# Letting the first gathers of a layer depend on 30 of 32 units' rows

## The chip, the cores and the metric

One core of a Trainium2 chip runs the whole program. TensorE (PE) multiplies matrices; its weight loads are listed apart as PEld. VectorE (DVE), ScalarE (ACT) and GpSimd (POOL) do the rest, and SyncE (SP) and POOL issue DMAs, which 16 DMA engines carry out. Each engine works through its own instruction list in the order in which the program was written. The metric is the time of one execution on the device, in microseconds (us).

## The reference

`x` holds 8 graphs' features for the same 2048 nodes, 128 numbers per node. `adj` says which nodes are neighbours; it is sparse: 34928 of the 2048 x 2048 entries are set, about 17 per node. Four layers follow each other: attention with 8 heads, graph attention, attention, graph attention.

```python
# attention layer, per node n over its neighbours m
scores = einsum('bnhd,bmhd->bhnm', Q, K) / sqrt(16);  scores = where(adj == 0, -inf, scores)
x = layer_norm(h + softmax(scores) @ V @ Wo + bo);  x = layer_norm(x + relu(x @ W1 + b1) @ W2 + b2)
# graph layer
h = x @ W;  e = leaky_relu((h @ a_src)[:, :, None] + (h @ a_dst)[:, None, :]);  e = where(adj == 0, -inf, e)
x = layer_norm(x + softmax(e) @ h)
```

A node's result in one layer needs the previous layer's result of all its neighbours.

## The kernel before, in words

**Units and slots.** The nodes are cut into 32 units of 64 nodes, each unit into two groups of 32. The edges of a group are written one per slot. A unit has nine tiles of 128 slots: four pairs of tiles (one tile of each pair per group, `t` = 0 to 3) and a shared ninth tile (`t` = 4), which takes what a group has beyond 512 edges, the first group from the front and the second from the back. `block_list` and `unit_list` (from L1027 and L1108) build these lists from `adj` on the chip: for each slot the index of the neighbour (`idx`), the node that owns it (`owner`) and a one-hot matrix (`hot`). An unused slot gets an index outside the table and is skipped. If a list overflows, the program runs a dense version (`failed`, `net`).

**Tables.** After a unit has finished a layer, `project` (L1390) makes its rows for the next layer: keys and values for attention, projected features for a graph layer. `store` (L1464) writes them to that layer's table in DRAM, a DMA that SP issues (L1470; L1467 for layer 0). `gather` (L1540) then fetches, by POOL's indirect DMAs (L1547), the rows of the slots of one unit's tile; a pair of tiles takes two such DMAs. Each gather reads the whole table, so the first gather of a layer waits for the stores of all 32 units.

**Attention layer** (`attention`, L1569), per unit and tile: PE spreads queries to slots (`qe`, L1620), DVE multiplies with the gathered keys (L1632) and sums (L1639), ACT takes the exponential (L1649), POOL or DVE multiplies the values with it (L1658), PE adds per node (L1690). `after_attention` is the rest of the layer: a chain of products, normalisations and transpositions. **Graph layer** (`graph`, L1790): PE spreads the nodes' scores to slots (`ps_te`, L1803), DVE adds the gathered ones (L1866, L1873), ACT takes the exponential (L1878), DVE makes weights (L1888), PE adds (L1904) into a bank `q` for even units and into `acc` and `sums` for odd ones. `after_graph` is the rest.

**Buffers.** `kv` (gathered rows) has 6 buffers, each of which holds one pair's gathers in an attention layer and four gathers in a graph layer; `hot` has 3, `te` 2, `x` 4. In PSUM there are one `q`, one `acc`, one `sums` and two `m`. The last unit of a layer is worked on in two halves (`in_halves`, L1701); `bank` (L1331) takes `m` for the first half and the `q` bank for the second.

**Order.** No engine's order is written out. Every step is an `op` with a cost per engine, a key and the cells that it reads and writes. `Plan.order` (L666) plays the program through with these costs and writes the instructions down in the order in which it started them; among steps that are ready on an engine the lowest key goes first. Layer n's keys begin at 1000 n, a unit adds 5, a tile 1; gathers are 6 or 12 lower than the tile that they serve. `kv`, `hot`, `x`, `q_sb` and `acc` are handed out strictly in order of keys (`BY_KEY`, L53): a later step can't take a buffer before an earlier one has.

Of the kernel before, what the change touches and what calls it, by code (L numbers as in the profile page):

```python
# [9 lines left out]
F32 = mybir.dt.float32  # L10
# [10 lines left out]
P = 128  # L21
H = 8
# [19 lines left out]
WIDE = DEG + 5  # L42
QB = 4
# [7 lines left out]
    "cand": 2, "aux": 3, "unit_aux": 2, "some": 2, "rank_e": 2, "pick": 1,  # L51
}
# [712 lines left out]
class Sparse:  # L765
# [15 lines left out]
    def __init__(self, ctx, tc, x, xt, xk, adj, w, out):  # L781
# [22 lines left out]
        self.late = False  # L804
# [13 lines left out]
        self.table = [Cell() for _ in LAYERS]  # L818

# [12 lines left out]
        self.ends = self.const.tile([P, self.NU, 2], F32, name="ends")  # L832

# [13 lines left out]
    def constants(self):  # L847
# [67 lines left out]
        for p in range(2):  # L915
            nc.gpsimd.memset(self.same_unit[p * UNIT : (p + 1) * UNIT, p * UNIT : (p + 1) * UNIT], 1.0)
        self.middle = const.tile([P, P], F32, name="middle")
# [109 lines left out]
    def block_list(self, adj, i):  # L1027
# [38 lines left out]
        aux = cell("aux", [P, WIDE])  # L1066
        some = cell("some", [P, DEG])

        def largest(e):
            c = cand.tile.rearrange("p q c -> p (q c)")  # L1070
            for r in range(DEG // 8):
                top = aux.tile[:, 8 * r : 8 * r + 8]
                e.max(out=top, in_=c)
                if r < DEG // 8 - 1:
                    e.match_replace(out=c, in_to_replace=top, in_values=c, imm_value=0.0)
            e.tensor_scalar(
                some.tile, aux.tile[:, 0:DEG], 0.0, 0.0, ALU.is_gt, ALU.add, accum_out=aux.tile[:, DEG + 4 : WIDE]
            )
            e.tensor_reduce(self.seen[:, 1, i : i + 1], aux.tile[:, 0:DEG], axis=mybir.AxisListType.X, op=ALU.add)

# [3 lines left out]
        def places(e):  # L1084
            deg = aux.tile[:, DEG + 4 : WIDE]
            for c, (w, x) in enumerate(
# [5 lines left out]
                    (self.upto, deg),  # L1092
                    (self.same_unit, deg),
# [6 lines left out]
        def ends(e):  # L1100
            e.copy(aux.tile[:, DEG : DEG + 4], ps.tile[:, 0:4])
            e.copy(self.seen[:, 2:4, i], ps.tile[:, 4:6])

        op({"ACT": 0.45}, ends, key + 0.3, reads=[ps], writes=[aux])
        for p in range(2):
            self.unit_list(2 * i + p, p, aux, key + 5 * p)

    def unit_list(self, u, p, block_aux, key):  # L1108
        op, cell = self.op, self.cell
        ps = cell("m", [P, CH], name="ps_aux")  # L1110
        aux = cell("unit_aux", [P, 2, DEG + 3])
        ends = Cell()
# [4 lines left out]
            lambda e: e.matmul(ps.tile[:, 0:WIDE], lhsT=self.to_unit[p], rhs=block_aux.tile, start=True, stop=True),  # L1117
# [7 lines left out]
        def split(e):  # L1125
# [3 lines left out]
            e.mul(ends.tile[:, 1:2], ps.tile[:, DEG + 4 : WIDE], 0.5)  # L1129

# [15 lines left out]

        ps_l = cell("m", [P, 2 * TG, DEG + 3], name="ps_l")

        def parts(e):
            for t in range(TG):  # L1150
# [6 lines left out]
                )  # L1157
            e.matmul(
# [7 lines left out]
        op({"PE": 1.0}, parts, key, reads=[hot, aux], writes=[ps_l])  # L1166
# [57 lines left out]
    def parts(self, u):  # L1224

        for hf in range(2):
            yield slice(hf * UNIT, (hf + 1) * UNIT), slice(u * UNIT, (u + 1) * UNIT), hf

# [29 lines left out]
    def fetch(self, n, u, key):  # L1258
# [39 lines left out]
        )  # L1298
        self.op(
# [13 lines left out]
    def in_half(self, v, made):  # L1313

        self.blocks, self.made, self.at, self.plan.share = range(2 * v, 2 * v + 2), made, 0, 0.55
# [5 lines left out]
    def rows(self, tag, shape, axis, unit, name=None):  # L1321
# [3 lines left out]
        if self.at == len(self.made):  # L1325
            self.made.append(self.cell(tag, shape, name=name))
        cut = (slice(None),) * axis + (slice(self.blocks.start * unit, self.blocks.stop * unit),)
        self.at += 1
        return Part(self.made[self.at - 1], lambda t: t[cut])

    def bank(self, name, shape=None):  # L1331

        shape = shape or [P, len(self.blocks) * P]
        if self.made is None or not self.blocks.start:
# [55 lines left out]
    def project(self, n, u, x, key, of=None, shares=()):  # L1390
# [73 lines left out]
        def store(e):  # L1464
# [8 lines left out]
            {"SP": 0.9 if n else 0.45}, store, key, reads=[rows], joins=[self.table[n]], dma=P * half * 4  # L1473
# [66 lines left out]
    def gather(self, n, u, t, width, key, kv, rows, writes, shares=()):  # L1540

        tiles = 1 if t == TG - 1 else 2

        def start(e):
            for j in range(tiles):
# [4 lines left out]
                    in_=self.tables[n],  # L1550
                    in_offset=bass.IndirectOffsetOnAxis(ap=self.idx[:, u, col : col + 1], axis=0),
                    bounds_check=self.N - 1,
# [7 lines left out]
            reads=[self.table[n], self.idx_at[u]],  # L1560
# [8 lines left out]
    def attention(self, n):  # L1569
# [3 lines left out]
        for u in range(self.NU):  # L1573
            base = n * STRIDE + u * TG
            x, hot = self.fetch(n, u, base - 12)
            ps = cell("m", [P, CH], name="ps_q")

            def queries(e, ps=ps, x=x):
                for b in range(hb):
                    cols = slice(b * P, (b + 1) * P)  # L1580
                    e.matmul(ps.tile[:, cols], lhsT=x.tile[:, cols], rhs=L["Wq"], start=True, stop=True)

            q = cell("q_sb", [P, CH])
            op({"PE": 1.1}, queries, base - 4, reads=[x, self.weights_at[n]], writes=[ps], holds=[q])
            op({"ACT": 0.6}, lambda e, q=q, ps=ps: e.copy(q.tile, ps.tile), base - 4, reads=[ps], writes=[q])
            acc = cell("acc", [P, CH])
            sums = cell("sums", [P, hb * H])
            for t in range(TG):
                key = base + t
                kv = cell("kv", [P, KV])  # L1590
                self.gather(
                    n,
                    u,
                    t,
                    2 * width,
                    key - 6,
                    kv,
                    lambda kv, j: kv[:, j * 2 * width : (j + 1) * 2 * width],
                    writes=[kv],
                )  # L1600

                tiles = 1 if t == TG - 1 else 2


                def part(kv, k, tiles=tiles):
                    rows = kv.tile[:, 0 : tiles * 2 * width].rearrange("p (q k c) -> p q k c", k=2, c=CH)
                    return rows[:, :, k, :]

                def exps(kv, tiles=tiles):
                    return kv.tile[:, 4 * width : 4 * width + tiles * heads]  # L1610

                qe = cell("q", [P, 2, 2, CH], name="qe")

                def spread(e, t=t, qe=qe, q=q, hot=hot, tiles=tiles):
                    for j in range(tiles):
                        for hf in range(2):
                            at = (2 * hf + j) * GROUP

                            rows = slice(at, at + GROUP * (3 - tiles))
                            e.matmul(  # L1620
                                qe.tile[:, j, hf, :],
                                lhsT=hot.tile[rows, t * P : (t + 1) * P],
                                rhs=q.tile[rows, :],
                                start=True,
                                stop=True,
                            )

                op({"PE": 1.2}, spread, key - 6, reads=[q, hot, self.table[n]], writes=[qe])

                def multiply(e, kv=kv, qe=qe, part=part, tiles=tiles):  # L1630
                    k = part(kv, 0)
                    e.tensor_tensor(k, qe.tile[:, 0:tiles].rearrange("p j h c -> p (j h) c"), k, ALU.mult)  # L1632

                op({"DVE": 1.12 * tiles}, multiply, key, reads=[qe], writes=[kv])
                s = cell("s", [P, 2 * heads])

                def reduce(e, kv=kv, s=s, part=part, tiles=tiles):
                    k = part(kv, 0).rearrange("p q (c d) -> p q c d", d=HD)
                    e.tensor_reduce(  # L1639
                        s.tile[:, 0 : tiles * heads].rearrange("p (q c) -> p q c", q=2 * tiles),  # L1640
                        k,
                        axis=mybir.AxisListType.X,
                        op=ALU.add,
                    )

                op({"DVE": 1.12 * tiles}, reduce, key, reads=[kv], writes=[s])

                def exp(e, out, s=s, tiles=tiles):
                    e.activation(out, s.tile[:, 0 : tiles * heads], AF.Exp, scale=HD**-0.5)  # L1649

                op({"ACT": 0.32}, lambda e, kv=kv, exp=exp, exps=exps: exp(e, exps(kv)), key - 4, reads=[s], writes=[kv])

                by_vector = t == TG - 1 and (n or u % 2) or n and u % 4 == 0 and t == 2

                def weigh(e, kv=kv, w=None, part=part, exps=exps, tiles=tiles):
                    v = part(kv, 1).rearrange("p q (c d) -> p q c d", d=HD)
                    w = (exps(kv) if w is None else w[:, 0 : tiles * heads]).rearrange("p (q c) -> p q c", q=2 * tiles)
                    e.tensor_tensor(v, v, w.unsqueeze(3).to_broadcast([P, 2 * tiles, heads // 2, HD]), ALU.mult)  # L1658

                if by_vector:  # L1660
                    ps = cell("m", [P, CH], name="ps_e")
                    op(
                        {"ACT": 0.32},
                        lambda e, ps=ps, exp=exp, tiles=tiles: exp(e, ps.tile[:, 0 : tiles * heads]),
                        key - 4,
                        reads=[s],
                        writes=[ps],
                    )
                    op(
                        {"DVE": 1.14 * tiles},  # L1670
                        lambda e, kv=kv, ps=ps, weigh=weigh: weigh(e, kv, ps.tile),
# [406 lines left out]
```

## Time and profile before

| what | value |
|---|---|
| median of 3 runs | 3018.71 us (3015.15 to 3028.6) |
| the profiled execution | 3037.61 us, span 3035.9 us, mean granted PE clock 0.882 |
| busy share of the span | PE 78%, DVE 76%, POOL 70%, PE weight loads 47%, ACT 46% |
| moved by DMA | 1022.92 MB, mean 337 GB/s |
| POOL's indirect gathers | 1152, of 1037 ns mean on POOL |
| first gather of layers 0, 1, 2, 3 | at 130.84, 1188.73, 1661.90, 2598.85 us |
| table stores of L1470, L1467 | 192 DMAs (two per unit), 32 DMAs |

Busy time is from one profiled execution; a share over the whole span averages over layers with different limits. A number in square brackets after an instruction in the timeline is the time for which its engine stood still before it, with what ended that.

### The profile page before, as it was taken

The numbers are of one execution on the slowest core, as the hardware profiler recorded it, in microseconds if no ns is written. First come the engines' busy times: TensorE is split into PE (matmuls) and PEld (weight loads), VectorE is DVE, ScalarE is ACT, GpSimd is POOL, SyncE is SP. The second block draws the span as 40 slices with busy tenths as digits, with TensorE's granted clock in tenths as the row PEclk, the third lists the DMA queues.
The fourth block names the chain that finished last, engine by engine and source line by source line (L and its number), as shares of the span: only waits on it lengthen the run. The fifth ranks groups of instructions, "written<-read, shape, count | busy, mean of one in ns | idle before, by whom it ended". The sixth has DMA issues, their size and how long they took to land. (4 is left out here: it accounts for less than half of the span.)

```text
span 3035.9 us, 60069 instructions
## 1 busy us (share of the span) xinstructions
PE 2383.0 (78%) x22044; PEld 1429.6 (47%) x22044; DVE 2306.6 (76%) x3744; ACT 1409.6 (46%) x4789; POOL 2139.0 (70%) x1455
## 2 busy tenths in 40 slices
PE   7877888788888786888886778878888878677775
PEld 6633444444433334666664233334334334566664
DVE  6788999987897785555553988888988988566665
ACT  4635554445544442555553234444445434344453
POOL 1277887687888773766663878878887885577774
PEclk8779998899998887899889799999999999777787
DMA  7778889798898884999997988988989885799996
GB/s 286 290 281 334 345 320 344 301 344 303 329 339 337 306 309 142 406 409 404 394 408 279 372 322 352 382 348 349 369 353 364 339 347 222 285 402 407 399 399 256
DMA packets 248494, 1022.92 MB, mean 337 GB/s; under 512 B 39232, under 2 KB 53312, under 8 KB 176288
## 3 DMA queue, kind: packets, MB, share of 16 engines
q0 software_dynamic: 166464, 864.44, 73.5%
q1 hardware_dynamic: 81728, 154.55, 14.0%
q8 instruction: 177, 2.90, 0.4%
q14 instruction: 125, 1.02, 0.1%
HBM read 978.59 MB, written 88.08 MB: 351 GB/s over the span
## 5 line engine op out<-in xcount | busy, mean ns | idle before, releaser
L1547 POOL DMA_INDIRECT kv<-table,idx x1152 | 1194.6, 1037 | 700.9 <-issue 314.3
L1658 POOL TENSOR_TENSOR kv<-kv 128x2048 f32<-128x2048 f32 (+1 forms) x260 | 931.2, 3595 | 55.2 <-ACT kv L1649 51.2
L1632 DVE TENSOR_TENSOR kv<-qe,kv 128x2048 f32<-128x2048 f32 (+1 forms) x320 | 662.3, 2070 | 169.1 <-DMA kv<-table,idx 110.8
L1639 DVE TENSOR_REDUCE s<-kv 128x128 f32<-128x2048 f32 (+1 forms) x320 | 660.0, 2062 | 7.6 <-DVE kv L1632 0.5
L1620 PE MATMUL qe<-q_sb,hot 32*128 32x512 f32 (+1 forms) x2304 | 399.3, 694 | 204.3 <-DVE kv L1632 202.0
L1690 PE MATMUL acc<-kv,hot 128*32 128x512 f32 (+1 forms) x2304 | 372.6, 660 | 60.0 <-POOL kv L1658 43.9
L1904 PE MATMUL acc_q<-kv,w 128*32 128x129 f32 (+1 forms) x4608 | 219.8, 328 | 134.7 <-DVE w L1888 104.9
L1888 DVE TENSOR_TENSOR w<-hot,e 128x512 f32<-128x512 f32 (+1 forms) x384 | 221.3, 598 | 52.8 <-ACT e L1878 52.0
L1620 PEld LDWEIGHTS qe<-q_sb,hot 32*128 32x128 f32 (+1 forms) x2304 | 106.9, 196 | 327.1 <-DVE kv L1632 269.1
L1904 PEld LDWEIGHTS acc_q<-kv,w 128*32 128x32 f32 (+1 forms) x4608 | 171.5, 135 | 172.3 <-DVE w L1888 100.1
L1649 ACT ACTIVATE kv<-s 128x128 f32<-128x128 f32 (+1 forms) x320 | 95.1, 298 | 336.7 <-DVE s L1639 225.9
L1866 DVE TENSOR_TENSOR e<-te,kv 128x16 f32<-128x16 f32 (+1 forms) x320 | 58.9, 184 | 227.5 <-DMA kv<-table,idx 225.1
L1484 ACT ACTIVATE junk<-ps_c 128x128 f32<-128x128 f32 x492 | 136.1, 277 | 162.8 <-PE ps_c L1372 137.0
L1348 ACT COPY trows<-ps_p 128x512 f32<-128x512 f32 (+1 forms) x238 | 113.3, 478 | 190.1 <-PE ps_p L1412 102.0
L1690 PEld LDWEIGHTS sums<-kv,hot 128*32 128x32 f32 (+1 forms) x2304 | 90.3, 121 | 215.3 <-issue 212.8
L1878 ACT ACTIVATE e<-e 128x16 f32<-128x16 f32 (+1 forms) x320 | 66.7, 212 | 248.2 <-DVE e L1873 246.1
L1904 PE MATMUL acc<-kv,w 128*32 128x129 f32 (+1 forms) x2304 | 119.9, 309 | 76.7 <-DVE w L1888 70.1
L1372 PE MATMUL ps_c<-centre,r 128*128 128x128 f32 x1008 | 150.8, 295 | 28.8 <-DVE r L1740 18.4
L1372 PEld LDWEIGHTS ps_c<-centre,r 128*128 128x128 f32 x1008 | 130.1, 201 | 73.2 <-DVE r L1740 36.7
L1382 PE MATMUL ps_f<-x,W 128*128 128x512 f32 (+1 forms) x256 | 149.2, 667 | 13.0 <-ACT x L1527 9.1
L1690 PEld LDWEIGHTS acc<-kv,hot 128*32 128x32 f32 (+1 forms) x2304 | 55.4, 115 | 203.6 <-issue 106.2
L1770 PE MATMUL ps_y<-hidden,W 128*128 128x512 f32 (+1 forms) x256 | 144.8, 652 | 5.9 <-ACT hidden L1760 3.0
(205 smaller groups left out, 4038.4 us busy)
## 6 DMA issues: line engine op xcount, KB each, us to landing
x<-xd SPq DMA_DIRECT2D x96, 256.0 KB
xd<-xnew SPq DMA_DIRECT2D x93, 256.0 KB
kv<-table,idx POOLq DMA_INDIRECT x1152
table<-trows SPq DMA_DIRECT2D x128, 130.0 KB
kv<-adj_dram SPq DMA_DIRECT2D x16, 1024.0 KB
table<-trows SPq DMA_DIRECT2D x32, 512.0 KB
table<-trows SPq DMA_DIRECT2D x64, 256.0 KB
kv<-xk_dram SPq DMA_DIRECT2D x8, 1024.0 KB
```

What stands on the lines that cost most here:

```text
L1372: e.matmul(ps.tile[:, cols], lhsT=flat(x.tile)[:, cols], rhs=self.centre, start=True, stop=True)
L1382: lambda e: e.matmul(ps.tile, lhsT=w, rhs=x.tile, start=True, stop=True),
L1484: e.activation(self.junk, x, AF.Square, scale=P**-0.5, accum_out=var.tile[:, b, 1:2])
L1547: e.indirect_dma_start(out=rows(kv.tile, j), out_offset=None, in_=self.tables[n], in_offset=bass.IndirectOffsetOnAxis(ap=self.idx[:, u, co ...
L1620: e.matmul(qe.tile[:, j, hf, :], lhsT=hot.tile[rows, t * P : (t + 1) * P], rhs=q.tile[rows, :], start=True, stop=True,)
L1632: e.tensor_tensor(k, qe.tile[:, 0:tiles].rearrange("p j h c -> p (j h) c"), k, ALU.mult)
L1639: e.tensor_reduce(s.tile[:, 0 : tiles * heads].rearrange("p (q c) -> p q c", q=2 * tiles), k, axis=mybir.AxisListType.X, op=ALU.add,)
L1658: e.tensor_tensor(v, v, w.unsqueeze(3).to_broadcast([P, 2 * tiles, heads // 2, HD]), ALU.mult)
L1690: e.matmul(out[rows, :], lhsT=hot.tile[:, col : col + GROUP * (3 - tiles)], rhs=rhs[:, 2 * j + hf, :], start=(t == 0), stop=(t == TG - 1),)
L1770: lambda e, f=f, ps=ps: e.matmul(ps.tile, lhsT=L["W2"][:, f, :], rhs=hidden.tile[:, f, :], start=(f == 0), stop=(f == FFN // P - 1),),
L1888: e.tensor_tensor(w.tile[:, :, j : j + tiles, :].rearrange("p x j c -> p j x c"), oh[:, j : j + tiles].unsqueeze(2).to_broadcast(shape), e ...
L1904: e.matmul(acc(b)[at : at + GROUP * (3 - tiles), :], lhsT=w.tile[:, hf * hb + b, j : j + 3 - tiles, :].rearrange("p j c -> p (j c)"), rhs= ...
```

## The change

In the lists of units 0 to 3 (`LATE = 4`), edges from the last 128 nodes (units 30 and 31) are no longer in the pairs: they go to the shared ninth tile. So the pair gathers of these units need only the first 1920 rows of a table. They get a table cut to these rows, and wait for units 0 to 29 only; units 30 and 31 report their stores to a second cell, `rest`, which all other gathers wait for as well. Graph layers take the work in another order: pairs of units 0 to 3, the ninth tiles of units 0 to 3, then unit after unit, the ninth tile of each following unit first or last as before. Attention layers keep their order (`sequence(0)`). In the half-by-half end of a layer ahead of a graph layer, the second half takes `m` banks (`tight`), so that `q` is free.

```diff
+LATE = 4
+PAIRS = TG - 1
+    def at(self, n, u):
+        return self.table[n] if u < self.NU - 2 else self.rest[n]
+    def sources(self, n, u, t):
+        return [self.table[n]] if u < LATE and t < PAIRS else [self.table[n], self.rest[n]]
...
-            {"SP": 0.9 if n else 0.45}, store, key, reads=[rows], joins=[self.table[n]], dma=P * half * 4
+            {"SP": 0.9 if n else 0.45}, store, key, reads=[rows], joins=[self.at(n, u)], dma=P * half * 4
...
+        nodes = self.N - P if u < LATE and t < PAIRS else self.N
-                    in_=self.tables[n],
+                    in_=self.tables[n][0:nodes],
-                    bounds_check=self.N - 1,
+                    bounds_check=nodes - 1,
-            reads=[self.table[n], self.idx_at[u]],
+            reads=[*self.sources(n, u, t), self.idx_at[u]],
...
+    def sequence(self, late):
+        for part in (range(PAIRS), range(PAIRS, TG)):
+            yield from ((u, t) for u in range(late) for t in part)
+        for u in range(late, self.NU):
+            yield from ((u, t) for t in range(TG))
...
+            if u < LATE:
+                t, at = i, u * 2 * PAIRS + 2 * i if i < PAIRS else LATE * 2 * PAIRS + u
+                key = base + i if i < PAIRS else n * STRIDE + LATE * TG - 2 + u / LATE
+            else:
+                t = i if u % 2 == 0 else (i - 1) % TG
...
-        if self.made is None or not self.blocks.start:
+        if self.made is None or not self.blocks.start or self.tight:
             return self.cell("m", shape, name=name)
...
+        self.tight = n < len(LAYERS) - 1 and LAYERS[n + 1] is not MHA
```

Building the lists takes more for units 0 to 3: the edges from the last 128 nodes are counted (`largest`), their places worked out (`late_places`, six DVE instructions of one column each, one matmul, one ACT copy), and their slots marked in the ninth tile's one-hot matrix. The marking is done again whenever a graph layer rebuilds `hot`:

```diff
+    def late_places(self, i, aux, ps, key):
...
+            e.tensor_scalar(begin, ps.tile[:, 4:5], float(PAIRS * P), None, ALU.max)
+            e.scalar_tensor_tensor(more, ps.tile[:, 5:6], deg, begin, ALU.add, ALU.subtract)
...
+    def late_targets(self, e, out, u):
+        e.activation(out, self.slot[:, GS - P : GS], AF.Abs, bias=self.late_ends[:, u, 0:1])
...
+        if u < LATE:
+            after = self.cell("late", [P, P])
...
+                e.scalar_tensor_tensor(shared, after.tile, self.late_ends[:, u, 1:2], shared, ALU.is_le, ALU.add)
```

The bodies of the tile loops of `attention` and `graph` are otherwise moved, not changed; the opening of a unit becomes a function of its own (`opened`, `opened_graph`).

## The prediction

> **What bounds the kernel now.** I read the page's slices first, then the busy time by stages, then POOL's waits, then the timeline of SP and POOL at each layer change. A layer gathers rows that every unit of the layer before may have written, so the changes are the places where transfers can run dry. Busy time by stage (length, then PE, PE weight loads, DVE, ACT, POOL busy with instruction counts, granted clock, DMA share, GB/s):
> ```profile
> 1160.00:1188.00 28.00, 20.19 (x88) 13.09 (x86) 15.44 (x49) 9.74 (x34) 0.00 (x0) 0.87 0.18 49
> 1188.00:1210.00 22.00, 10.54 (x144) 8.44 (x146) 7.14 (x25) 2.00 (x7) 16.70 (x16) 0.50 0.84 288
> ...
> 1250.00:1600.00 350.00, 283.46 (x4389) 230.27 (x4386) 188.49 (x665) 192.24 (x679) 233.42 (x228) 0.89 1.02 405
> ...
> 2555.00:2598.00 43.00, 30.57 (x178) 19.01 (x174) 29.03 (x72) 16.79 (x64) 0.00 (x0) 0.95 0.16 50
> ...
> 2640.00:3000.00 360.00, 272.38 (x4608) 230.50 (x4608) 241.37 (x791) 170.38 (x684) 274.56 (x256) 0.78 1.02 400
> ```
> Inside a graph layer (1250 to 1600, 2640 to 3000) the DMA engines are full, 1.02 at 400 to 405 GB/s, and no engine is: the graph layers are bound by the gathers. Just before each, they are nearly empty (0.18 and 0.16) and POOL, which issues the gathers, does nothing. A transfer-bound stage that starts t earlier ends t earlier. POOL's waits say what it stood for (total, times, longest):
> ```profile
> POOL kv L1547 <- DMA table<-trows: 87.7, 2, 44.0
> ...
> POOL kv L1547 <- DMA hot<-hots: 37.5, 1, 37.5
> ```
> Two waits of 43.7 and 44.0 us for the last table store (the two graph layers) and one of 37.5 at layer 2. The last names another load, but the last stores (issued 1654.70 to 1657.53) land at the same moment. Only the part of each wait after unit 29's store can go. SP's and POOL's timelines at the first change:
> ```profile
> 1157.78 1.09 SPq L1470 DMA_DIRECT2D table<-trows  x2
> ...
> 1181.69 1.09 SPq L1470 DMA_DIRECT2D table<-trows  x2
> ...
> 1185.11 1.09 SPq L1470 DMA_DIRECT2D table<-trows  x2
> ```
> ```profile
> 1188.73 1.03 POOL L1547 DMA_INDIRECT kv<-table,idx  x1 [43.68 <-DMA table<-trows]
> ```
> These are units 29, 30 and 31. From the issue of the last store to the first gather is 1188.73 - 1185.11 = 3.6 us; so unit 29's rows are there at 1161.4.
>
> **What the change releases.** T0 is unit 29's store plus 3.6 us.
> - Layer 0 to 1: 1188.73 - 1161.4 = 27.3 us.
> - Layer 2 to 3: unit 29's store is issued at 2574.56, T0 = 2578.2, the first gather now is at 2598.85: 20.7 us.
> - Layer 1 to 2: unit 29's at 1650.45, T0 = 1654.0, first gather 1661.90: 7.9 us. Here the order stays unit by unit and kv buffers are given in order of keys, so unit 0's ninth tile bars unit 1. Four pairs, 8 gathers at the 1.29 us between POOL's starts, are 10.3 us of issue: enough to cover 7.9.
> - Layer 0's start: the last three stores are issued at about 123.5, 123.87 and 126.94: 3.4 us.
> POOL's last own multiplication is over at 1145.0 and 2554.9, before either T0, so no gather is queued ahead of one. From the adjacency I count the ninth tiles of units 0 to 3: 89, 61, 56 and 92 edges of 128, so the lists hold.
>
> **How much of it a graph layer keeps.** In its new order come 32 pair gathers (units 0 to 3), four ninths, then unit 4. Gathers are spaced 1.29 us, so the ninths leave at T0 + 41.3, and this is the deadline of units 30 and 31. kv has 6 buffers of 4 gathers; 24 fit at once, and units 0 and 1 free theirs from about T0 + 12 (first gather to first score 1195.59 - 1188.73 = 6.9, score to last matmul 3.4, from the second pair 2.7 later), ahead of need. But unit 2 accumulates in the bank that unit 0 holds until its ninth tile is in. Units 2 and 3 keep 4 buffers, the ninths 1, unit 4's first gathers 1: all six. POOL stands from T0 + 40 x 1.29 = 51.6 until unit 2's first two pairs are added: unit 0's ninth 41.3 + 5.6 landing + 3.4 = 50.3, its scaling 1.5 (1638.10 to 1639.55), two groups of matmuls of 1.95 each: 55.7. That is 4 us without new gathers; bounds 0 (if transfers are still queued) to 10 (if unit 3 repeats it); I take **5 per graph layer**.
>
> **What delays units 30 and 31.**
> - The second half of unit 31 moves from the spare q bank to the two m banks. I add from the timeline how long it held q: 1.25, 2.0, 3.57, 1.14, 1.93, 1.22, 2.94, 3.2, 1.03, 1.33 = 19.6 us. Over two banks this is 9.8 us; bounds 0 (m idle) to 19.6 (one behind the other); I take 9.8.
> - PE: 8 pairs of units 0 and 1 at 1.95 are 15.6 us more beside the 20.2 busy of the 28. 35.8 fits the lengthened 37.8, nothing added.
> - DVE: graph scores now stand among the tail's work and may wait for their rows. The row:
> ```profile
> DVE e L1866 <- DMA kv<-table,idx: 225.1, 193, 10.8
> ```
> That is 1.17 us a wait, 8 scores, 9.3 us. The Trainium skill ("TensorE: Matmul & The Clock Gate", section on the array of 32x32 sub-arrays) says VectorE and ScalarE are strict first-in, first-out; it speaks against the change, for whatever tail work is planned behind a score stands too. By the rule 9.3 are paid in full, more where several rows come late together; by the row, DVE is busy only 15.4 of 28 us in the tail and an idle DVE waits free: 0 to 9.3. I take the rule's end.
> - Stores: 3.6 us landing is measured beside idle DMA engines, and now gathers run. By the Trainium skill ("DMA: Bandwidth & Descriptors", section on queues, rings and completion order) each engine takes turns between queues, packet by packet, so the store of 266 KB gets half of 400 GB/s: +0.7 us. No row shows a store under gathers; the nearest, a gather landing after 8.8 us in the chain, would give +5. I take 0.7, as SP's and POOL's transfers are on separate queues of the page.
> Together 9.8 + 9.3 + 0.7 = 19.8. Layer 1: the stores land at T0 + 27.3 + 19.8 = 47.1, 5.8 past the deadline. Layer 3: T0 + 40.5, in time.
>
> **What it adds elsewhere.** Lists of units 0 to 3: DVE two small instructions and six of about 0.16 for each of two blocks (1.3 each), two 128x128 per unit (0.5): 4.6 us; ACT some 5 per unit (1.1): 4.4 us; PE under 2. DVE is busy 48.5 of the 66 us before layer 0's start, ACT 40.4, so between 0 and 4.6 shows; I set it equal to the 3.4 gained: **layer 0 gives 0**. POOL's five memsets (about 1 us at its start) lie before 42 idle us. In each graph layer ACT 0.3 and DVE 0.3 for four units: 2.4 us on engines with half their time idle; their hot tiles are prepared ahead; 0, and at most 2.4 if not.
>
> **The sum.** Layer 1: 27.3 - 5 - 5.8 = 16.5. Layer 2: 7.9. Layer 3: 20.7 - 5 = 15.7. Total 40.1. The profiled execution took 3037.6 (span 3035.9), so 2997.5 by its clock; the median of the runs is 18.9 lower, and the differences are stalls, not rates, so 3018.7 - 40 = **2979 us**.
>
> **Rivals.** Half a per cent, 15 us, is about what a measurement here can tell from no change.
> 1. The release happens but half is given back (0.22): units 2 and 3 hold buffers and unit 3 repeats the stall (10), the delay is 30 instead of 19.8, so layer 1 keeps 27.3 - 10 - 16 = 1, layer 3 20.7 - 10 - 9.4 = 1, layer 2 all 7.9, the list costs 0 to 1 more: about 3009. A milder form, one of the two, gives 2990 to 3000. For it: PE is 81% busy in layer 1, so a backlog drains slowly. Against: kv refills in four-gather steps.
> 2. It does better (0.10): no DVE wait lies ahead of tail work, transfers queued in the rings bridge the refill, PE's clock, 0.50 after the gap, stays up: 27.3 + 20.7 + 7.9 + 3.4 = 59, 2959. Against it: the shared m banks.
> 3. It doesn't do what it says (0.05): the gather still waits for all stores of the table, as its operand is the same tensor. Then only the costs are left, 3019 to 3028. Against: its rows are cut to the first 1920, and SP's stores of units 30 and 31 lie outside.
> 4. Slower (0.07): the tail of unit 31 is a chain of 11 matmul steps with 22 DVE and ACT steps between. If the issue order puts one group of graph matmuls (1.95) or one score wait (1.17) ahead of each, it grows by 21.5 + 25.7 + 9.8 = 57 us; stores at T0 + 84 and T0 + 78, 43 and 37 past the deadline; layers 1 and 3 lose 43 + 5 - 27.3 = 21 and 37 + 5 - 20.7 = 21; less 7.9: 3053. Past the deadline a graph layer gains 36.3 less the delay (27.3 + 41.3 - 27.3 - 5), so with layer 2's 7.9 the sign turns at a delay of 40 us. Against: the keys of a finishing layer are lower and go first when ready.
>
> **The numbers.** Likeliest case 0.56, 2979, own range 2967 to 2993. Faster by over 0.5% (below 3003.6): likeliest, better and most of rival 1: 0.82. Within 0.5%: the rest of rival 1 and part of 3: 0.10. Slower: 0.08. The range leaves out the worst of rivals 1, 3 and 4: 2955 to 3007.
>
> **What would show it.** First gathers of layers 1, 2 and 3 some 27, 8 and 20 us earlier relative to unit 31's old store, POOL's three long waits cut to 16, 30 and 23 us; DMA share above 0.8 between T0 and unit 31's store; a POOL wait of about 5 us for a unit 2 accumulation (10 in layer 1); unit 29's to unit 31's store stretched from 27 to 47 and 21 to 40. Wrong if the DMA share dips after T0 + 40 for over 15 us, if unit 29's own store slips, or if layers 0 and 2 change length by over 10 us inside.

## The result and the profile after

The changed kernel takes 2979.69 us (median of 4 runs, 2968.79 to 2981.53), the kernel before 3021.65 (4 runs beside them); the ratio is 0.9853, with a 95% interval of 0.982 to 0.9887. The forecast was 2979. In a later set of runs the ratio was 0.9874 (0.9842 to 0.9906).

The busy time by stages of the changed kernel (columns as before), around layer 1's start, layer 3's start, and inside layer 1:
```profile
1144.00:1159.00 15.00, 12.59 (x100) 6.98 (x98) 13.39 (x28) 7.64 (x29) 1.10 (x1) 0.93 0.20 54
1159.00:1185.00 26.00, 21.50 (x249) 13.81 (x250) 16.38 (x52) 10.21 (x35) 19.81 (x20) 0.87 0.92 342
1185.00:1205.00 20.00, 10.36 (x106) 8.40 (x105) 6.25 (x21) 2.56 (x12) 13.21 (x14) 0.72 1.03 409
1205.00:1225.00 20.00, 13.45 (x183) 11.84 (x184) 12.50 (x52) 9.37 (x35) 10.29 (x11) 0.59 0.74 253
1225.00:1245.00 20.00, 20.00 (x340) 16.64 (x344) 14.28 (x52) 15.91 (x61) 15.43 (x16) 1.00 1.00 372
1245.00:1600.00 355.00, 277.92 (x4508) 227.89 (x4496) 185.89 (x664) 197.07 (x703) 238.79 (x229) 0.92 1.03 404
...
2532.00:2558.00 26.00, 21.45 (x210) 12.07 (x211) 17.90 (x53) 10.81 (x34) 20.16 (x18) 0.87 0.82 299
2558.00:2580.00 22.00, 13.68 (x184) 10.73 (x184) 9.37 (x33) 4.01 (x17) 14.81 (x16) 0.92 1.03 412
2580.00:2600.00 20.00, 12.36 (x176) 11.07 (x178) 11.50 (x46) 8.05 (x31) 9.88 (x10) 0.58 0.74 249
```
While units 30 and 31 are still being finished, the DMA engines are now at 0.92 and 0.82, where they were at 0.18 and 0.16. The inside of layer 1 runs as it did (1.03, 404 GB/s). New is a dip to 0.74 some 45 us after the first gather, in both graph layers. POOL's timeline says what it is:
```profile
1159.40 1.02 POOL L1647 DMA_INDIRECT kv<-table,idx  x1 [14.30 <-DMA table<-trows]
...
1204.39 0.98 POOL L1647 DMA_INDIRECT kv<-table,idx  x1 [3.14 <-DMA table<-trows]
...
1221.58 1.05 POOL L1647 DMA_INDIRECT kv<-table,idx  x1 [6.97 <-PE acc_q L1984]
```
The first line is unit 0's first gather. The second is the first ninth tile, which stood 3.14 us for the rows of unit 31. The third stood 6.97 us until unit 2's first pairs were added and a `kv` buffer came free. In steps of 5 us the DMA share is 0.93, 0.87, 0.84 and 0.34 between 1205 and 1225, so the hole is deep only at its end. In layer 3 the same two waits are 2.92 and 7.67. SP's timeline, units 29, 30 and 31:
```profile
1155.75 1.09 SPq L1569 DMA_DIRECT2D table<-trows  x2
...
1186.89 1.09 SPq L1569 DMA_DIRECT2D table<-trows  x2
...
1193.64 1.28 SPq L1339 DMA_DIRECT2D xd<-xnew  x2
1196.44 1.24 SPq L1569 DMA_DIRECT2D table<-trows  x2
```
The `xd` line writes unit 31's result to DRAM. From unit 29's store to the first gather 1159.40 - 1155.75 = 3.65 us have passed, where it was 31.0. From unit 29's to unit 31's it is 40.7 us, where it was 27.3.

From these two timelines I take five stretches per kernel, in us: from the issue of unit 29's store to the layer's first gather ("gap"), and from first gather to unit 29's store of the next layer (layer 1) or to the end (layer 3). Each is from one profiled execution.

| kernel | gap 1 | gap 2 | gap 3 | layer 1 | layer 3 | ratio |
|---|---|---|---|---|---|---|
| before | 31.0 | 11.5 | 24.3 | 461.7 | 437.1 | 1 |
| change | 3.7 | 6.6 | 3.7 | 465.1 | 447.1 | 0.9853 |
| change again | 3.7 | 6.6 | 3.7 | 466.0 | 447.8 | 0.9874 |
| lists only | 31.2 | 12.1 | 28.6 | 462.0 | 438.4 | 0.9994 |
| lists and m banks | 37.9 | 11.7 | 37.0 | 462.2 | 436.1 | 1.0073 |
| all but the release | 38.4 | 14.3 | 36.1 | 465.6 | 441.3 | 1.0092 |
| two early units | 3.7 | 5.5 | 3.7 | 477.3 | 459.3 | 0.9923 |
| three early units | 3.7 | 5.7 | 3.7 | 471.3 | 454.1 | 0.9856 |

Unit 29's store is not a fixed point of a layer, though. At the end of layer 2 it moved against the work around it. Before, with the last product that adds values (L1690) and unit 29's store:
```profile
2567.11 0.25 PE L1690 MATMUL sums<-kv,hot 128*64 128x32 f32 x4
...
2574.56 1.09 SPq L1470 DMA_DIRECT2D table<-trows  x2
```
In the change:
```profile
2528.94 1.09 SPq L1569 DMA_DIRECT2D table<-trows  x2
...
2539.64 0.26 PE L1780 MATMUL sums<-kv,hot 128*64 128x32 f32 x4
```
The store came 7.2 us after the last such product and comes 11.0 us ahead of it now. So a second table measures from that last product. "Start" is the time from a layer's last product to the next layer's first gather (negative when the gather is first), "layer" the time from first gather to last product.

| kernel | start 1 | layer 1 | start 2 | layer 2 | start 3 | layer 3 |
|---|---|---|---|---|---|---|
| before | 31.2 | 449.4 | 23.8 | 905.5 | 31.5 | 416.7 |
| change | 2.3 | 459.2 | 12.4 | 908.8 | -7.2 | 427.3 |
| lists and m banks | 36.6 | 449.5 | 24.4 | 912.3 | 37.3 | 415.8 |
| all but the release | 37.1 | 459.8 | 20.2 | 907.3 | 36.5 | 420.9 |
| release in graph layers only | 2.3 | 458.5 | 19.9 | 899.7 | 4.0 | 425.2 |
| release in attention layers only | 36.6 | 457.5 | 12.8 | 909.4 | 33.7 | 421.6 |
| two early units | 2.3 | 467.3 | 15.5 | 901.0 | -7.1 | 439.1 |
| three early units | 2.4 | 458.7 | 18.2 | 899.8 | -6.7 | 433.7 |

### The profile page after: what moved, and what is told of

Read it like the earlier page. It is cut to its first block, busy times and chain, and to the rows that moved or that the text cites. A ratio compares the mean times of both kernels' runs of the same rounds, so it can differ in the third digit from the quotient of the medians.

```text
span 2979.8 us, 60236 instructions
## 1 busy us (share of the span) xinstructions
PE 2346.3 (79%) x22064; PEld 1401.5 (47%) x22064; DVE 2302.5 (77%) x3775; ACT 1414.5 (47%) x4821; POOL 2138.6 (72%) x1459
## 3 DMA queue, kind: packets, MB, share of 16 engines
q14 instruction: 126, 1.03, 0.1%
## 5 line engine op out<-in xcount | busy, mean ns | idle before, releaser
L1984 PE MATMUL acc_q<-kv,w 128*32 128x129 f32 (+1 forms) x4608 | 202.1, 308 | 121.5 <-DVE w L1968 96.9
L1984 PEld LDWEIGHTS acc_q<-kv,w 128*32 128x32 f32 (+1 forms) x4608 | 158.2, 126 | 151.5 <-DVE w L1968 109.5
L1447 ACT COPY trows<-ps_p 128x258 f32<-128x258 f32 (+1 forms) x240 | 113.8, 476 | 187.9 <-PE ps_p L1511 103.7
L1481 PE MATMUL ps_f<-x,W 128*128 128x512 f32 (+1 forms) x264 | 155.7, 674 | 23.5 <-ACT hidden L1877 16.2
L1471 PEld LDWEIGHTS ps_c<-centre,r 128*128 128x128 f32 x1024 | 132.3, 202 | 74.1 <-DVE r L1857 33.7
```

Of the source, the lines that this page charges most:

```text
L1471: e.matmul(ps.tile[:, cols], lhsT=flat(x.tile)[:, cols], rhs=self.centre, start=True, stop=True)
L1481: lambda e: e.matmul(ps.tile, lhsT=w, rhs=x.tile, start=True, stop=True),
L1984: e.matmul(acc(b)[at : at + GROUP * (3 - tiles), :], lhsT=w.tile[:, hf * hb + b, j : j + 3 - tiles, :].rearrange("p j c -> p (j c)"), rhs= ...
```

## The experiments

Each kernel was timed beside the kernel before, in 4 to 14 executions. The theory: the gain is the earlier start of gathers, and all else in the change costs. The rival: the new issue order is the gain.

**All but the release.** Every gather waits for 32 units; lists, order and banks stay.
```diff
-        return [self.table[n]] if u < LATE and t < PAIRS else [self.table[n], self.rest[n]]
+        return [self.table[n]] if u < 0 and t < PAIRS else [self.table[n], self.rest[n]]
-        nodes = self.N - P if u < LATE and t < PAIRS else self.N
+        nodes = self.N - P if u < 0 and t < PAIRS else self.N
```


> The changed kernel, but every gather waits for the stores of all 32 units, as before; lists, order of the graph layers and the m banks for the tail stay. Theory (the earlier release is the gain; order and banks only cost): the gain is gone, and the refill stall of unit 2 (7 us of POOL measured per graph layer) and a tail up to 10 us longer ahead of each graph layer remain: 3020 to 3050 us, ratio to the kernel before 1.00 to 1.01. Rival (the gain comes from the new issue order in layers 0 and 2, whatever the gathers wait for): 2980 to 2995, ratio 0.987 to 0.992.

Measured: 3050.54, ratio 1.0092 (1.0064 to 1.0121), half a microsecond above the theory's range. The rival is out. The release is worth 1.0092 - 0.9853 = 2.4%, some 72 us, and what comes with it costs 0.9%. Layer 1's first gather in this kernel:
```profile
1184.30 1.03 POOL L1647 DMA_INDIRECT kv<-table,idx  x1 [48.98 <-DMA table<-trows]
```
POOL stands 48.98 us instead of 43.68.

**Release in the graph layers only.**
```diff
-        nodes = self.N - P if u < LATE and t < PAIRS else self.N
+        nodes = self.N - P if u < LATE and LAYERS[n] is GAT and t < PAIRS else self.N
```
The condition in `sources` is changed alike.

> The changed kernel with the early release in the two graph layers only; in the attention layers all gathers wait for 32 units. Theory: loses what layer 2's start (and layer 0's 3 us) brought. By the profile the release opens 7.9 us there, but unit 31's last product then waits 12 us for the q bank, so little is lost: 2978 to 2990. Rival (layer 2's early start is worth its whole 8 us or more): 2988 to 2995.

Measured: 2985.43, 0.989 (0.9865 to 0.9916), within the theory's range. The attention layers' release is worth 0.4%, which these intervals don't tell from nothing.

**Release in the attention layers only**: the same edit with `LAYERS[n] is MHA`.

> The changed kernel with the early release in the two attention layers only; graph layers keep their new order, but all their gathers wait for 32 units. Theory: the graph layers' release is the larger part, so this is near the kernel without any release: 3010 to 3045, first graph gather about 30 us after unit 29's store and more. Rival (issue order and attention layers are the gain): 2980 to 2995.

Measured: 3040.02, 1.006 (1.0035 to 1.0085). The graph layers' release, the difference to the whole change, is 2.1%, 62 us. Added alone to the kernel without release it brings 2.0% (1.0092 - 0.989), so the two ways of taking it agree.

**Two early units; three early units.** `EARLY` takes the place of `LATE` in the graph layers' order, sources and rows; lists as in the change.
```diff
+EARLY = 2
-        for u, i in self.sequence(LATE):
+        for u, i in self.sequence(EARLY):
-            if u < LATE:
-                t, at = i, u * 2 * PAIRS + 2 * i if i < PAIRS else LATE * 2 * PAIRS + u
-                key = base + i if i < PAIRS else n * STRIDE + LATE * TG - 2 + u / LATE
+            if u < EARLY:
+                t, at = i, u * 2 * PAIRS + 2 * i if i < PAIRS else EARLY * 2 * PAIRS + u
+                key = base + i if i < PAIRS else n * STRIDE + EARLY * TG - 2 + u / EARLY
```


> The changed kernel with the graph layers' early order and release for units 0 and 1 only (lists unchanged; attention layers unchanged). The ninths now come 16 gathers x 1.29 = 20.6 us after the first gather, while the rows of units 30 and 31 are there 45 to 47 us after it. Theory (the number of early gathers sets the deadline): POOL stands about 24 us for the last stores in each graph layer, but units 0 and 1 have banks of their own, so the 7 us refill stall and the 3 us wait fall away: 14 us lost per graph layer, 3000 to 3012. Rival (the transfers catch up later, since no stage is bound by the gathers alone): 2978 to 2990.

> The changed kernel with the graph layers' early order and release for units 0 to 2 (lists unchanged). Ninths 24 x 1.29 = 31 us after the first gather, last rows 45 us after it: POOL stands 14 us for them, but unit 2 alone holds 2 kv buffers, so the 7 us refill stall goes, and the 3 us wait is part of the 14. Theory: 4 us per graph layer lost against four units, 2982 to 2992, between two and four units. Rival (tail and refill differ enough that three is best): below 2978.

Measured, two: 2994.48, 0.9923 (0.9896 to 0.9951). Three: 2982.7, 0.9856 (0.9828 to 0.9884). POOL's timeline with two, then with three:
```profile
1189.68 0.98 POOL L1648 DMA_INDIRECT kv<-table,idx  x1 [19.73 <-DMA table<-trows]
```
```profile
1201.42 0.99 POOL L1648 DMA_INDIRECT kv<-table,idx  x1 [9.73 <-DMA table<-trows]
```
In layer 1 the wait for the last rows is 19.73 and 9.73 us, in layer 3 20.48 and 12.44, and the long wait for unit 2 is gone in both. By the second table two units make layer 1 8.1 us longer than the change and layer 3 11.8 (expected 14 each). Three leave layer 1 as it is (-0.5) and make layer 3 6.4 longer (expected 4 each), and the whole time can't be told from that of four. In layer 1 this is about what POOL stands more or less than the 10.1 us of the change. So the number of early gathers sets the deadline, as thought. The total with two units came out between theory and rival; layer 2 was 8 to 9 us shorter in both profiles, which isn't explained.

**Lists only; lists and m banks.** No release (the two edits of the first experiment) and the old order, with `EARLY` for `LATE` throughout the graph layers' order; `tight` false in the first (shown), as in the change in the second.
```diff
+EARLY = 0
...
-        for u, i in self.sequence(LATE):
+        for u, i in self.sequence(EARLY):
...
-        self.tight = n < len(LAYERS) - 1 and LAYERS[n + 1] is not MHA
+        self.tight = False
```

> Only the lists of the change: units 0 to 3 have their late edges in the ninth tile, but every gather waits for all 32 units, the graph layers run in the old order and the tail uses the spare q bank as before. Theory: the lists cost 0 to 5 us, so the 31 us that the kernel without any release lost against the kernel before come from the new order and the m banks: 3019 to 3026. Rival (the lists and the rewritten loops are dear): 3035 to 3050.

> The lists-only kernel (old order, every gather waits for 32 units) plus one thing: the last unit's second half takes the m banks ahead of a graph layer. Theory (the kernel without release lost 31 us, by its segments 19 in the two stretches from unit 29's store to the first graph gather and 8 inside the graph layers): banks alone cost the 19, so 3039 to 3048, ratio 1.005 to 1.008, and the stretch grows from 31 and 24 us to 38 and 36. Rival (the graph layers' new order costs most of it): 3025 to 3032, stretches unchanged.

Measured: 0.9994 (0.9975 to 1.0013) and 1.0073 (1.0048 to 1.0099). The lists cost nothing that can be measured. The banks cost 0.8%. The two kernels differ in the banks alone, and gap 1 is 6.7 and gap 3 8.4 us longer in the second. POOL's waits for this kernel:
```profile
POOL kv L1648 <- DMA table<-trows: 97.3, 2, 49.4
```
Two waits of 87.7 in all have become 97.3. What the first experiment has beyond this kernel is the graph layers' order: by the second table they are 10.3 and 5.1 us longer there, and POOL stands 8.97 and 6.49 us for unit 2. In the whole time, 1.0092 against 1.0073, this is within the noise.

**Spreads after all stores; m banks ahead of every layer.** In the trace of the change I saw a hole at layer 2's start:
```profile
1644.77 2.05 PE L1509 MATMUL ps_p_q<-Wkv,xnew 128*128 128x256 f32 x4 [11.98 <-DVE kv L1722]
```
Unit 31's last product waits 12 us for the q bank. The first spread of layer 2 has taken it, and gives it back when its gather has landed and been multiplied. So unit 31's rows are stored at 1647.46, and unit 0's ninth tile is gathered at 1658.51, 17 us after the end of the gather before it. Two ways out:
```diff
-            op({"PE": 1.2}, spread, key - 6, reads=[q, hot, *self.sources(n, u, t)], writes=[qe])
+            op({"PE": 1.2}, spread, key - 6, reads=[q, hot, self.table[n], self.rest[n]], writes=[qe])
```
```diff
-        self.tight = n < len(LAYERS) - 1 and LAYERS[n + 1] is not MHA
+        self.tight = n < len(LAYERS) - 1
```


> The changed kernel, with one difference in the planner only: the matmuls that spread queries to slots in attention layers count as ready when all 32 units are stored, as before. So they can't take the q bank while unit 31's second half still needs it. Theory (at layer 2's start the first spread holds q until its gather has landed, unit 31's last product waits 12 us behind it, and POOL's ninth-tile gather comes 17 us late): the hole closes and layer 2 gets back 5 to 12 us: 2968 to 2975, gap after the 8th gather of layer 2 below 8 us. Rival (the hole is filled again later, since layer 2 is not bound at its start): 2978 to 2985.

> The changed kernel, with the m banks for the second half also ahead of layer 2 (before, only ahead of graph layers). Theory: unit 31 needs no q bank ahead of layer 2, so its last product doesn't wait 12 us for the first spread; against it the two m banks carry more, some 5 to 10 us. Net 0 to 8 us better: 2972 to 2980. Rival (bank pressure outweighs it): 2983 to 2992.

Measured: 2983.54, 0.9854 (0.9826 to 0.9881), and 2983.32, 0.9867 (0.9841 to 0.9893). In the first the hole did close:
```profile
1646.94 0.99 POOL L1647 DMA_INDIRECT kv<-table,idx  x1 [4.02 <-issue]
```
It is 4 us, and the time didn't move. My theory of 5 to 12 us falls: from first gather to last product layer 2 took 906.0 us here and 908.8 in the change, so most of the hole is made good within the layer. Nor did the second way reach the 2972 to 2980 that its theory had.

**Scores after all stores.** The planner holds the graph layers' first scores back, gathers start as early as in the change.
```diff
-            op({"DVE": 0.38}, score, key - 1, reads=[te, now], writes=[e8], shares=[kv])
+            op({"DVE": 0.38}, score, key - 1, reads=[te, now, self.rest[n]], writes=[e8], shares=[kv])
```


> The changed kernel, but the planner lets the graph layers' first scores start only after all 32 units are stored; gathers start as early as in the change. So no graph work stands among the tail's on DVE, ACT and PE. Theory (graph work among the tail costs it 6 and 11 us): unit 29's to unit 31's store shrinks from 41 and 43 us to about 35 and 32, as in the kernel without release; but kv frees nothing until then, so POOL stands after 24 gathers (31 us) for about 10 us: 2982 to 2995. Rival (the tail is longer because transfers share the DMA engines): the stretch stays 41 and 43.

Measured: 2989.95, 0.9895 (0.9868 to 0.9922), within the expectation. SP's timeline at the first change:
```profile
1153.66 1.09 SPq L1569 DMA_DIRECT2D table<-trows  x2
...
1187.42 1.24 SPq L1569 DMA_DIRECT2D table<-trows  x2
```
The stretch from unit 29 to 31 is 33.8 us, 7 less than in the change. At layer 3 it is 40.1, only 3.4 less, where I expected 11 less. So graph work among the tail explains the first and not the second, which is taken up below.

**The change again; three units and spreads together.** The first has no edit, the second joins two edits above.

> The changed kernel once more, beside these runs: ratio 0.982 to 0.989; a second profile for the stretches. Theory: the boundary and graph stretches repeat within 2 us, and the 15 us by which layer 2 was shorter than in the kernel before do not (runs differ there). Rival: layer 2 is shorter again by about 15 us, so the release or the plan changed it.

> Three early units in the graph layers and the spreads after all 32 units' stores together. Alone neither was told from the change. Theory: together no more than 5 us from the change, 2975 to 2988. Rival (two small gains that add up): 2965 to 2974.

Measured: 2982.64, 0.9874 (0.9842 to 0.9906), and 2993.2, 0.991 (0.988 to 0.9939). The stretches repeat within 1 us. Layer 2, from its first gather to unit 29's store, is 896.6 us again, against 912.7 before, so this part of the rival holds. But to its last product it takes 907.4, against 905.5: it is unit 29's store that comes sooner, not the end of the layer. The join is slower than both expectations; in it layer 2 took 910.1. No version beat the change.

## Why the prediction was right, step by step

The mechanism held: without the release the gain is gone, and what comes with it costs. The sum of its terms held less well than its total. By the first table the stretches at the layer changes and inside the graph layers add up to -27.3 + 3.4 - 4.9 - 20.6 + 10.0 = -39.4 us, where -40.1 was forecast; the medians differ by 42. But this leaves out layer 2, shorter by 15 up to unit 29's store. By the second table the starts gave 28.9, 11.4 and 38.7 us, 79.0 in all where 55.9 was forecast; the graph layers took back 9.8 and 10.6, where 10.8 and 5 was forecast, and layer 2 3.3. With 0.4 each up to layer 0's last product and after layer 3's this is the 56 us between the two profiled executions. 16 us is how far the profiled execution of before lay above its median; no run shows in which stretch it stood. So that 2979 was met within a microsecond is in part luck.

- **The release.** The first gather now follows unit 29's store by 3.7 us in layers 1 and 3, so the gaps shrink by 27.3 and 20.6, as forecast. For layer 2 7.9 forecast, 4.9 measured: its first gather came 6.6 us after unit 29's store was issued, not 3.6. That store took SP 1.98 us to issue instead of 1.09, and the wait ended with a small load that SP had issued behind it.
- **Unit 29 came sooner: the step that was left out.** I let unit 29's store stand where it was in the work around it. At the end of layer 2 it comes 18.2 us earlier against the last product. It comes 10.4 to 11.0 us ahead of that product in six profiles with the attention layers' release (the change twice, attention layers only, two units, three units, scores held back). It comes 0.3 us behind it in seven others: those without that release, those with the spreads held back, and the one with m banks ahead of every layer. So it comes with the order that the planner wrote; why it wrote it so isn't shown. This, and not a faster layer, is what made layer 2 look shorter. To its last product it took 899.7 to 912.3 us in all 14 profiles, with and without release alike.
- **The m banks**: 9.8 forecast, from the time for which the second half held q. Banks alone lengthened the gaps by 6.7 and 8.4.
- **Graph work among the tail**: 9.3 forecast as the rule's end. In layer 1, from the kernel without release to the change, unit 29's to unit 31's store went from 34.7 to 40.7, 6.0 us between the row's end (0) and the rule's, and holding the scores back gave them back. In layer 3 it went from 32.4 to 43.5. There 40.6 stands already in the kernel with release in the attention layers only, where no gather of layer 3 is early: unit 29's store had moved. Against that kernel, and against the one with scores held back, graph work costs some 3 us. With the release in the graph layers only, where the store had not moved, it costs 6.8 (39.2 against 32.4).
- **Stores under gathers: the term that was mis-sized.** I took +0.7 us, half of the bandwidth for the store's 266 KB, from the rule that the DMA engines take turns between queues, packet by packet (the Trainium skill, "DMA: Bandwidth & Descriptors", section on queues, rings and completion order), and set aside the nearest row, which gave +5. In the change the last store takes 1204.39 - 1196.44 = 8.0 us from issue to gather, and 7.3 in layer 3. With two or three early units, whose gathers have all been issued some time before, it takes 3.7 to 3.9. So gathers in flight cost it some 4 us. The trace says where they go. From 1197.1 to 1200.7, just after the store's issue, the queues (packets, MB, share of the 16 engines) show:
```profile
q0 software_dynamic: 317, 1.17, 79.2%
q1 hardware_dynamic: 311, 0.31, 24.5%
```
q1, SP's queue, moves about as many packets as the gathers on q0. But its packets are mostly the 1024-byte ones of `xd`, the gathers' are of 4160 bytes, so it gets a fifth of the bytes and not half. And these 256 KB of `xd`, issued ahead of the store, are still under way for 4.2 us after the store's issue; with two early units they had ended 0.5 us before it. The store's own packets, of 2080 bytes, end 6.5 us after its issue instead of 2.7. Turns by packet, as the trace counts packets, fit what is seen; my working left out the size of the packets and what stood ahead on the same queue.
- **The deadline.** Rows of unit 31 at T0 + 47.1 and T0 + 40.5 forecast; 45.0 and 47.0 measured, 3.1 and 2.9 us past the ninths. In layer 1 two errors offset each other: the stretch to unit 31's store grew by 13.4 us, not 19.1, and the store by 4.3, not 0.7. For layer 3 I had said in time. The tail from the last product to unit 31's store grew by less than 5 us there (27.7 to 32.5). But T0 hangs on unit 29's store, and that had moved away from the last product by 18.
- **The refill of kv**: 5 forecast, 7.0 and 7.7 measured, and at the place forecast, unit 2's first addition. A seventh kv buffer, which would test it, wasn't tried; nor was leaving q to the tail in the new order, since unit 0 holds that bank until its ninth tile is in.
- **What the two waits cost.** 10.8 and 5 forecast. By the second table the graph layers are 9.8 and 10.6 us longer than before, and POOL stood 10.1 and 10.6 in the two waits: in these layers a delay of the gathers was a delay of the layer. The first table has only 3.4 for layer 1, because unit 29's store follows that layer's last product by 5.8 us instead of 12.4.
- **Layer 0**: 0 forecast. The first gather came at 120.9 to 127.3 us in nine profiles with the release there and at 128.7 to 135.2 in five without, some 8 us earlier (I had 3.4, and read even that wrong: the last three stores span 123.01 to 126.94, 3.9 us). Yet the layer's last product came at 1154.1 us on average in the nine and at 1154.0 in the five. So nothing was kept of it: the 0 was right, but not shown to be for the reason given, the cost of the lists.
- **Its own signs.** The DMA share and the place of the refill came as forecast. Of POOL's three long waits, forecast at 16, 30 and 23 us, 14.3, 27.4 and 6.3 are left. Two signs of being wrong came up too: the dip after T0 + 40 lasted some 20 us, though it is deep in only 5, and layer 2 changed by 15 us as measured to unit 29's store.

## What to carry to other kernels

Where a stage bound by transfers follows one that isn't, the gap between the last-but-some write and the first read can be worth its whole length, but only if the work that is released is long enough to reach past the last writes: two early units left POOL 20 us short, three 10 to 12, four 3. Where the stage isn't bound by transfers it may be worth nothing: layer 0 (mean DMA share 0.87 between 200 and 1100 us) began to gather 8 us earlier and ended when it did before. Ask what the reordering holds on to meanwhile (here PSUM banks and row buffers), for this cost 0.9% and was paid from a gain of 2.4%. For a store that must land among heavy reads, count what stands ahead of it on its own queue, and compare the size of its packets with that of the reads. And measure a layer between marks that the plan can't move: one unit's store is no such mark.

## What the runs showed of the hardware that was not expected

The time from a table store's issue to a gather that may read it doubles with indirect gathers in flight: 3.7 to 3.9 us with them issued well before, 7.2 to 8.0 in the two profiles of the change, with POOL issuing one every 1.29 us until shortly before. SP's own issue of the two DMAs changed little (1.09 to 1.24 us). Beside gathers with packets of 4160 bytes, SP's queue moved about one packet for each of theirs (311 to 317 in 3.6 us), but 0.31 MB to their 1.17: here the small packets got a fifth of the bytes, not half.
